# Softplus of dt in a state-space scan: its last sum moved from GpSimd to VectorE, its bias moved into the product

## The chip, the cores and the metric

The kernel runs on one core of a Trainium2 chip. A core has five engines that run beside each other, each with a queue of its own: TensorE (PE, matrix products, with a separate weight load, PEld), VectorE (DVE), ScalarE (ACT), GpSimd (POOL) and SyncE (SP, which here issues nearly all transfers). SBUF is the working memory of 128 partitions; PSUM is the smaller memory that PE writes its products to. The metric is the device time of one execution in microseconds (us), and the time of a kernel is the median of its runs. All numbers are fp32 throughout.

## The reference

Four images of 384 channels and 32 x 32 pixels pass two layers. The first begins with a selective scan (a state-space model) over each image in four directions k, with 16 states for each channel. Cut to what matters:

```python
xs = _cross_scan(x)                                   # 4 directions, each (384, 1024)
x_dbl = einsum('bkdl,kcd->bkcl', xs, x_proj_weight)   # 44 rows: 12 dts, 16 B, 16 C
dts = einsum('bkrl,kdr->bkdl', dts, dt_projs_weight)  # 12 -> 384
A = -exp(A_logs)
dt = softplus(dts + dt_projs_bias[None, :, :, None])
# for each position l:   h = h * exp(dt * A) + (dt * u) * B ;  y = sum over n of h * C
ys = ys + Ds * u
x = x + gelu(layernorm(_cross_merge(ys)))
```

After it come a mixture of four experts (each token takes two of them, hidden width 1536), an attention layer with eight heads, and a last two-layer product. In this document these three, with the routing and combining around the experts, are called the tail of an image.

## The kernel before

**The scan.** Work is cut into 32 units: image b (4), direction k (4) and half i (2) of the 1024 positions, 512 positions in each. A unit is cut into three chunks c of 128 channels. For a chunk, `chunk` (L388) loads dt and dt*u from memory in a layout where a partition is a pair of channel and state (`dtr`, L401 to L406), and then, four times, for 4 of the 16 states (g), and for two pairs (q): POOL multiplies dt*u by B (`bx`, L419), ACT takes the exponential of dt times A into a PSUM tile (`da`, L428, two buffers), DVE runs the recurrence along the positions (the scan, L433). The product with C is made by POOL for q = 0 (L447) and by DVE for q = 1 (L440). PE sums over states with a selection matrix into `acc` (L454), and DVE adds that to `y` (L281, L285). There are six buffers of `bx`, which come free when PE has read them.

**The projection.** `project` (L292) prepares the next unit while the present one is scanned: it is a generator that `scan_layer` steps forward once after each group of four states. It multiplies the input with `wx` to 44 rows (`xd_ps`, L317), copies them to SBUF (`xd`, L321), sends the B and C rows through memory to be spread over partitions (`bcs`), and then for each chunk calls `begin`: PE multiplies 12 rows with `wdt` into the PSUM tile `dt_ps` (L344), and softplus follows. It is written as relu(v) + ln(1 + e) with e = exp(-|v|), v being the product plus the bias, and one term more. That term is the rounding error of 1 + e: `one_e` is the rounded sum 1 + e, and ln(1 + e) is better given by ln(one_e) - ((one_e - 1) - e). So the sum has four parts: relu, ln(one_e), -(one_e - 1) and e.

The first image and the others differ in how they sum it. For image 0, PE does it with four identity products (L357), since no other work claims PE then. For images 1 to 3 ACT makes relu in place in `dt_ps` (L349) and `one_e - 1` (L361); POOL makes the two differences (L374, L375), and DVE adds the last to `dt_ps` (L381). In both cases DVE then multiplies by the input (L382), ACT copies dt out of PSUM (L383), and SP sends both to memory (`dd`, L384 and L385), from where `chunk` loads them for the next unit. The bias comes in through the bias operand of ACT's Abs and Relu (L348, L349), from a column of the constants `cols`.

**PSUM.** `dt_ps`, `acc`, `xd_ps` and the two tiles of each layer norm share one tag with two buffers (`psum`, tag "ps").

**The order.** While image b is scanned, the tail of image b - 1 is put among its instructions: `between` calls `tail_batch`, with `route` (L603), `experts` (L836: L906 and L921 on PE), `combine` (L932: two diagonal tiles by POOL, L942, and 16 gathers by POOL, L951), `attention` (L989: L1030 and L1076 on PE) and `last_layers` (L1089). The program text doesn't fix the order of a queue: when the kernel is built, a scheduler works it out for every engine from the dependencies, from priorities and from its own estimate of each instruction's time. Each queue is then fixed. Three things in the text bind it further: in `project` the sums are placed behind the last POOL or DVE instruction of the state group before (`behind`), parts of the tail carry a higher priority, and the tail of image 3 has nothing beside it but what the tail of image 2 has left.

Of the kernel before, what the change touches and what calls it, by code (L numbers as in the profile page):

```python
# [9 lines left out]
F32 = mybir.dt.float32  # L10
I32 = mybir.dt.int32
AF = mybir.ActivationFunctionType
ALU = mybir.AluOpType
# [4 lines left out]
P = 128  # L18
B = 4
D = 384  # L20
DC = D // P
HW = 32
L = HW * HW
HF = 512
NH = L // HF

KG = 4
ORDER = (0, 1, 3, 2)
NS = 16
R = 12  # L30
XD = R + 2 * NS
# [28 lines left out]

_COLS = [
    ("alog", KG * NB * NG),
    ("dtb", KG * DC),
    ("ds", KG * DC),
    ("lnw", DC),
    ("lnb", DC),
# [22 lines left out]
class Room:  # L89


    def __init__(self, tc, ctx, name, bufs):
        self.tc, self.name, self.bufs = tc, name, bufs
        self.sb = ctx.enter_context(tc.tile_pool(name=name, bufs=1, reuse_waits="tile"))
# [14 lines left out]
def halves(i):  # L109
    return slice(i * HF, (i + 1) * HF)  # L110


class Body:
    def __init__(self, ctx, tc, a):
        self.tc, self.nc, self.a = tc, tc.nc, a
        nc = self.nc
        const = ctx.enter_context(tc.tile_pool(name="const", bufs=1))
        self.const = const


        nc.scalar.preload_act_table_set("natural_log_exp_and_others")
        self.cols = const.tile([P, NCOL], F32, tag="cols", name="cols")
        nc.scalar.dma_start(out=self.cols, in_=a["cols"])

        self.ident = const.tile([P, P], F32, tag="ident", name="ident")
        make_identity(nc, self.ident)
        self.ones = const.tile([P, P], F32, tag="ones", name="ones")
        nc.gpsimd.memset(self.ones, 1.0)
        self.eps5 = const.tile([P, 1], F32, tag="eps5", name="eps5")
        nc.gpsimd.memset(self.eps5, 1e-5)  # L130
        self.eps6 = const.tile([P, 1], F32, tag="eps6", name="eps6")
        nc.gpsimd.memset(self.eps6, 1e-6)

        self.minus1 = const.tile([P, 1], F32, tag="minus1", name="minus1")
        nc.gpsimd.memset(self.minus1, -1.0)

        self.c2sum = const.tile([P, 1], F32, tag="c2sum", name="c2sum")
        lo, hi = COL["c2"]
        nc.vector.tensor_reduce(self.c2sum, self.cols[:, lo:hi], AX.X, ALU.add)
# [42 lines left out]
    def scan_layer(self, x1, between):  # L182

        nc, tc, a = self.nc, self.tc, self.a
        with ExitStack() as ctx:
            wp = ctx.enter_context(tc.tile_pool(name="s_w", bufs=1))
# [2 lines left out]
            dap = ctx.enter_context(tc.tile_pool(name="s_da", bufs=2, space=PSUM))  # L189
            psum = ctx.enter_context(tc.tile_pool(name="s_ps", bufs=2, space=PSUM))  # L190

            wx = wp.tile([P, DC, KG, XD], F32, tag="wx", name="wx")
            nc.scalar.dma_start(out=wx, in_=a["wx"].rearrange("(c p) k m -> p c k m", p=P))
            nega = wp.tile([P, KG * NB * NG], F32, tag="nega", name="nega")
            lo, hi = COL["alog"]
# [57 lines left out]
            for n, unit in enumerate(units):  # L253
                b, k, i = unit
                fed, ahead = ahead, []
                project = iter(())
                if n + 1 < len(units):
                    nb = units[n + 1][0]
                    if nb not in us:
                        us[nb] = start(nb)  # L260
                    project = self.project(units[n + 1], us[nb], wx, work, dram, psum, ahead)
                    next(project)
# [4 lines left out]
                for c in range(DC):  # L267
# [5 lines left out]
                    if k % 2 == 0:  # L273
                        ys = y[:, c, halves(i)]
                        out = acc
                    else:
                        w = slice(i * (HW // NH), (i + 1) * (HW // NH))
                        ys = y[:, c, :].rearrange("p (h w) -> p h w", h=HW)[:, :, w]
                        out = acc.rearrange("p (w h) -> p h w", h=HW)
# [12 lines left out]
    def project(self, unit, u, wx, work, dram, psum, made):  # L292

        nc, a = self.nc, self.a
        b, k, i = unit
        by_cols = k % 2 == 1
        w = slice(i * (HW // NH), (i + 1) * (HW // NH))  # L300

        def part(c):
            if by_cols:
                return u[:, c, :].rearrange("p (h w) -> p w h", h=HW)[:, w, :]
            return u[:, c, halves(i)]

        def split(ap):
            return ap.rearrange("p (w h) -> p w h", h=HW) if by_cols else ap

        def k2(name, shape=(P, HF)):  # L310
            return work.tile([*shape], F32, tag="k2", name=name, bufs=6)

        wdt = k2("wdt", (R, D))
        nc.sync.dma_start(out=wdt, in_=a["wdt"][:, k, :])
        ps = psum.tile([P, HF], F32, tag="ps", name="xd_ps")
        for c in range(DC):
            nc.tensor.matmul(  # L317
                split(ps[:XD, :]), wx[:, c, k, :], part(c), start=(c == 0), stop=(c == DC - 1)
            )
        xd = k2("xd", (XD, HF))  # L320
        nc.scalar.copy(xd, ps[:XD, :])  # L321
        rows = dram.tile([2 * NS, HF], F32, tag="rows", name="rows")
        nc.sync.dma_start(out=rows, in_=xd[R:XD, :])
        view = rows.rearrange("(t g n) l -> n t g l", t=2, g=NG)
        bcs = []
        for g in range(NG):
            bc = work.tile([P, 2, HF], F32, tag="bcs", name="bcs", bufs=5)
            for n in range(NJ):
                nc.sync.dma_start(
                    out=bc[n * DB : (n + 1) * DB], in_=view[n, :, g].partition_broadcast(DB)  # L330
                )
            bcs.append(bc)

        dd = dram.tile([2, D, HF], F32, tag="dd", name="dd")
        made += [bcs, dd]
        yield  # L340

        def begin(c):
            ps = psum.tile([P, HF], F32, tag="ps", name="dt_ps")
            nc.tensor.matmul(ps, wdt[:, c * P : (c + 1) * P], xd[:R, :], start=True, stop=True)  # L344
            bias = self.col("dtb", k * DC + c)
            mag, one_e, lnw = k2("mag"), k2("one_e"), k2("lnw")
            relu = k2("relu") if b == 0 else ps
            nc.scalar.activation(mag, ps, AF.Abs, bias=bias)  # L348
            nc.scalar.activation(relu, ps, AF.Relu, bias=bias)  # L349
            nc.scalar.activation(mag, mag, AF.Exp, scale=-1.0)  # L350
            nc.scalar.activation(one_e, mag, AF.Identity, bias=1.0)
            nc.scalar.activation(lnw, one_e, AF.Ln)
            if b == 0:
                nc.scalar.activation(one_e, one_e, AF.Identity, bias=1.0, scale=-1.0)
                terms = [lnw, one_e, mag, relu]
                for t in terms:
                    nc.tensor.matmul(  # L357
                        ps, self.ident, t, start=(t is terms[0]), stop=(t is terms[-1])
                    )
            else:  # L360
                nc.scalar.activation(one_e, one_e, AF.Identity, bias=self.minus1)  # L361
            return ps, mag, one_e, lnw

        def behind(engine):
            if self.place_behind is None:
                return nullcontext()
            return self.tc.issue_after(self.place_behind[engine])

        for c in range(DC):
            ps, mag, one_e, lnw = begin(c)  # L370
            yield
            if b > 0:
                with behind("pool"):
                    nc.gpsimd.tensor_sub(mag, one_e, mag)  # L374
                    nc.gpsimd.tensor_sub(lnw, lnw, mag)  # L375
            yield
            d, du = mag, one_e
            rows = slice(c * P, (c + 1) * P)
            with behind("dve"):
                if b > 0:  # L380
                    nc.vector.tensor_add(ps, ps, lnw)  # L381
                nc.vector.tensor_mul(split(du), split(ps), part(c))  # L382
            nc.scalar.copy(d, ps)  # L383
            nc.sync.dma_start(out=dd[0, rows, :], in_=d)  # L384
            ins = nc.sync.dma_start(out=dd[1, rows, :], in_=du).ins  # L385
        made.append(ins)
# [602 lines left out]
    def attention(self, xc, sums, room):  # L989
# [68 lines left out]

        steps = [(t, i, j) for t in range(HEADS // 2) for i in range(NH) for j in range(MB)]
        made = [project(0)]  # L1060
        ahead = scores(0, made[0][0], 0, 0, None)
        atts = []
# [292 lines left out]
def layouts(inputs):  # L1355

    i = {k: np.asarray(v) for k, v in inputs.items()}

    def vec(v, lead):
        return np.moveaxis(v.reshape(*lead, P, -1), len(lead), 0).reshape(P, -1)  # L1360
# [2 lines left out]
        "alog": np.ascontiguousarray(  # L1363
            i["L0_conv_A_logs"].reshape(KG, NB, DB, NG, NJ).transpose(4, 2, 0, 1, 3)
        ).reshape(P, -1),
        "dtb": vec(i["L0_conv_dt_projs_bias"], (KG, DC)),
        "ds": vec(i["L0_conv_Ds"], (KG, DC)),
        "lnw": vec(i["L0_conv_ln_weight"], (DC,)),
        "lnb": vec(i["L0_conv_ln_bias"], (DC,)),
# [7 lines left out]
    arrays = {  # L1377
        "x": i["x"].reshape(B, D, L),
        "cols": np.concatenate([packed[n] for n, _ in _COLS], axis=1),
        "wx": i["L0_conv_x_proj_weight"].transpose(2, 0, 1),  # L1380
        "wdt": i["L0_conv_dt_projs_weight"].transpose(2, 0, 1),
        "wg": i["L0_ffn_gate_w"],
        "bg": i["L0_ffn_gate_b"],
        "w1": i["L0_ffn_w1"].reshape(NE, DC, P, HID).transpose(0, 2, 1, 3),
# [6 lines left out]
            axis=2,  # L1391
# [9 lines left out]
            axis=1,  # L1401
# [7 lines left out]
            axis=1,  # L1409
# [19 lines left out]
```

## Time and profile before

| what | value |
|---|---|
| median of 3 runs | 4389.3 us (4378.26 to 4389.32) |
| profiled execution, its own time | 4365.25 us |
| its span, first to last instruction | 4363.5 us |
| busy PE | 3382.3 us (78%) |
| busy POOL | 3049.6 us (70%) |
| busy DVE | 2919.3 us (67%) |
| busy ACT | 2504.0 us (57%) |
| mean granted clock of PE | 0.86 |
| DMA moved | 684.74 MB |

The profile is of one execution. A busy time is the union of an engine's instructions; a span's stretches are named by their start and end in us. In a row of the groups view stand the line of the kernel, the engine, the operation, output and inputs by the program's names, shapes, the count after an x, then busy time in us, mean ns of one, and the idle time of the engine just before these instructions with what ended it. A row of the waits view says who waited for whom, and then the total in us, how often, and the longest. A row of the stretches gives start and end, length, busy time of PE, weight load, DVE, ACT and POOL, each with a count, then the granted clock of PE, the share of the DMA engines and GB/s.

### The profile page before, as it was taken

To read this page: it belongs to the slowest core of one execution; us is meant where nothing else is said; L and a number is where in the kernel's file an instruction comes from. 1 tells how busy PE (TensorE), PEld (TensorE's weight loads), DVE (VectorE), ACT (ScalarE), POOL (GpSimd) and SP (SyncE) were. 2 spreads that over 40 slices of the span, in tenths; PEclk is the share of its full clock that TensorE was granted. 3 is DMA by queue.
4 is the path that set the end of the run, shared out by engine and by line. 5 is a ranking of instruction groups with operands and counts; after the bars stand their busy time and mean duration, and the time that the engine had idled before them with its cause. 6 is when DMAs were issued, how large, how long until landed. Compare 5 with 4: busy or idle time off the path is not lost. (4 is left out here: it accounts for less than half of the span.)

```text
span 4363.5 us, 46084 instructions
## 1 busy us (share of the span) xinstructions
PE 3382.3 (78%) x13436; PEld 1581.3 (36%) x13436; DVE 2919.3 (67%) x4331; ACT 2504.0 (57%) x4470; POOL 3049.6 (70%) x1475
## 2 busy tenths in 40 slices
PE   6545544379997895579997888579998799999896
PEld 2111111145553221235554322135554234666323
DVE  5888888967877868968787867968887740200102
ACT  4445545556665875466575777466666564343353
POOL 5999998898988968688898978789898831000100
PEclk7766776589997997779998999679999899999997
DMA  5444354577886534457779534457789434336200
GB/s 136 114 122 116 106 162 115 151 228 214 231 241 183 142 109 139 125 174 213 213 229 279 154 95 132 115 158 225 215 233 273 134 108 142 116 126 214 63 17 15
DMA packets 404756, 684.74 MB, mean 157 GB/s; under 512 B 50960, under 2 KB 206480, under 8 KB 404496
## 3 DMA queue, kind: packets, MB, share of 16 engines
q1 hardware_dynamic: 395184, 655.37, 51.9%
q0 software_dynamic: 8192, 25.17, 1.7%
q8 instruction: 108, 1.77, 0.2%
q14 instruction: 152, 1.25, 0.1%
q10 hardware_dynamic: 1120, 1.18, 0.1%
HBM read 561.47 MB, written 120.06 MB: 156 GB/s over the span
## 5 line engine op out<-in xcount | busy, mean ns | idle before, releaser
L419 POOL TENSOR_TENSOR bx<-dtr,bcs 128x1024 f32<-128x1024 f32 x768 | 1792.4, 2361 | 229.6 <-PE acc L454 118.7
L428 ACT ACTIVATE da<-dtr,nega 128x512 f32<-128x512 f32 x1536 | 1045.3, 690 | 945.8 <-DVE bx L440 564.3
L447 POOL TENSOR_TENSOR bx<-bx,bcs 128x1024 f32<-128x1024 f32 x384 | 903.1, 2359 | 179.1 <-DVE carry L444 74.3
L906 PE MATMUL h_ps<-xc,w 128*128 128x256 f32 (+1 forms) x3168 | 675.0, 368 | 60.8 <-DMA w<-in_w 18.7
L454 PE MATMUL acc<-bx,sel 128*32 128x512 f32 x3072 | 496.8, 697 | 289.2 <-POOL bx L447 232.4
L921 PE MATMUL y_ps<-w,hs 128*128 128x384 f32 x1824 | 643.2, 505 | 38.1 <-ACT hs L914 37.8
L906 PEld LDWEIGHTS h_ps<-xc,w 128*128 128x128 f32 x3168 | 556.1, 200 | 238.7 <-issue 112.8
L433 DVE TENSOR_TENSOR_SCAN bx<-da,carry,bx 128x512 f32<-128x512 f32 x384 | 474.7, 1270 | 129.3 <-ACT da L428 65.8
L433 DVE TENSOR_TENSOR_SCAN bx<-da,bx 128x512 f32<-128x512 f32 x384 | 453.3, 1210 | 117.1 <-POOL bx L419 59.2
L433 DVE TENSOR_TENSOR_SCAN da<-da,carry,bx 128x512 f32<-128x512 f32 x384 | 478.0, 1274 | 66.5 <-ACT da L428 60.9
L440 DVE TENSOR_TENSOR bx<-da,bcs 128x512 f32<-128x512 f32 x768 | 510.3, 680 | 3.7
L433 DVE TENSOR_TENSOR_SCAN da<-da,bx 128x512 f32<-128x512 f32 x384 | 456.2, 1219 | 63.3 <-ACT da L428 53.0
L921 PEld LDWEIGHTS y_ps<-w,hs 128*128 128x128 f32 x1824 | 350.0, 196 | 325.8 <-issue 78.2
L1036 ACT ACTIVATE ex<-s_ps 128x512 f32<-128x512 f32 x512 | 300.8, 592 | 156.6 <-PE s_ps L1030 154.4
L1030 PE MATMUL s_ps<-w 64*128 64x512 f32 x1024 | 307.9, 662 | 53.1 <-ACT ex L1036 51.8
L911 ACT ACTIVATE hs<-h_ps,bb 128x256 f32<-128x256 f32 (+1 forms) x528 | 201.0, 441 | 218.8 <-PE h_ps L906 218.4
L1076 PE MATMUL o_acc<-ex,vt 128*64 128x512 f32 x1024 | 287.0, 638 | 18.1 <-ACT ex L1036 11.5
L454 PEld LDWEIGHTS acc<-bx,sel 128*32 128x32 f32 x3072 | 80.0, 116 | 585.9 <-POOL bx L447 319.8
L942 POOL TENSOR_TENSOR diag<-ident,g_weight 128x1024 f32<-128x1024 f32 x8 | 15.0, 1893 | 345.6 <-PE xc_ps L889 331.0
L925 DVE TENSOR_TENSOR y<-y_ps,bb 128x384 f32<-128x384 f32 x76 | 41.7, 549 | 273.4 <-PE y_ps L921 273.4
L344 PE MATMUL dt_ps<-xd,wdt 12*128 12x512 f32 x192 | 123.2, 726 | 71.4 <-ACT mag L383 43.8
L1030 PEld LDWEIGHTS s_ps<-w 64*128 64x128 f32 x1024 | 82.8, 190 | 256.0 <-ACT ex L1036 206.0
(214 smaller groups left out, 3767.2 us busy)
## 6 DMA issues: line engine op xcount, KB each, us to landing
w<-in_w SPq DMA_DIRECT2D x352, 576.0 KB
dtr<-dd SPq DMA_DIRECT2D x1536, 128.0 KB
bcs<-rows SPq DMA_DIRECT2D x512, 128.0 KB
dd<-one_e SPq DMA_DIRECT2D x96, 256.0 KB
dd<-mag SPq DMA_DIRECT2D x96, 256.0 KB
rows<-zero SPq DMA_DIRECT2D x76, 192.0 KB
xs<-rows SPq DMA_DIRECT2D x32, 384.0 KB
made<-y SPq DMA_DIRECT2D x32, 384.0 KB
```

Source lines behind the costliest of these rows:

```text
L419: pool = nc.gpsimd.tensor_mul(bx, dtr[q][1], bc[:, 0].unsqueeze(1).to_broadcast([P, 2, HF])).ins
L428: nc.scalar.activation(da, dtr[q][0][:, j, :], AF.Exp, scale=nega[:, col : col + 1])
L433: nc.vector.tensor_tensor_scan(run(h), run(da), run(bx[:, j, :]), 0.0 if first else hold, ALU.mult, ALU.add,)
L440: dve = nc.vector.tensor_mul(bx[:, j, :], h, cg).ins
L447: pool = nc.gpsimd.tensor_mul(bx, bx, cg.unsqueeze(1).to_broadcast([P, 2, HF])).ins
L454: nc.tensor.matmul(acc[lo : lo + DB, :], sel, out[q][:, j, :], start=(g == 0), stop=(g == NG - 1),)
L906: nc.tensor.matmul(ps[:, r, :], w1[(f + r) // wf][:, c, (f + r) % wf * P : ((f + r) % wf + 1) * P], xc[:, c, :], start=(c == 0), stop=(c = ...
L911: nc.scalar.activation(hs[:, f + r, :], ps[:, r, :], AF.Identity, bias=bb[:, f + r : f + r + 1])
L921: nc.tensor.matmul(out[:, :D], hs[:, f, t * P : (t + 1) * P], w2[f // wf][:, f % wf, :], start=(f == 0), stop=(f == FC - 1),)
L1030: ins = nc.tensor.matmul(ps, w[rows, j * P : (j + 1) * P], w[rows, halves(i)], start=True, stop=True).ins
L1036: done.append(nc.scalar.activation(ex[:, o, :], ps, AF.Exp, scale=HD**-0.5, accum_out=sums[:, t, 2 * j + o, i : i + 1],).ins)
L1076: ins = nc.tensor.matmul(out[cols, :], made[t][1][:, j, cols], ex[:, o, :], start=(j == 0), stop=(j == MB - 1),).ins
```

## The change

The bias of dt enters through the product. `wx` gets a column of zeros, so that `xd` has a 45th row of zeros, to which ACT adds 1 as it copies (an Identity with a column of the identity matrix as its bias). `wdt` gets 32 rows of zeros, against the B and C rows, and the bias as its 45th row. The dt product runs over all 45 rows. The bias columns and the constant -1 are gone.

For images 1 to 3, ACT makes neither relu nor `one_e - 1`, and POOL makes no difference. DVE sums in three steps in `dt_ps`, each a scalar_tensor_tensor: max(v, 0) + lnw, then (one_e - 1) - that, then -that + e. Image 0 keeps its four products on PE and its relu.

```diff
-            wx = wp.tile([P, DC, KG, XD], F32, tag="wx", name="wx")
+            wx = wp.tile([P, DC, KG, XD + 1], F32, tag="wx", name="wx")
...
-        wdt = k2("wdt", (R, D))
+        wdt = k2("wdt", (XD + 1, D))
...
-                split(ps[:XD, :]), wx[:, c, k, :], part(c), start=(c == 0), stop=(c == DC - 1)
+                split(ps[: XD + 1, :]), wx[:, c, k, :], part(c), start=(c == 0), stop=(c == DC - 1)
...
-        xd = k2("xd", (XD, HF))
-        nc.scalar.copy(xd, ps[:XD, :])
+        xd = k2("xd", (XD + 1, HF))
+        nc.scalar.activation(
+            xd, ps[: XD + 1, :], AF.Identity, bias=self.ident[: XD + 1, XD : XD + 1]
+        )
...
-            nc.tensor.matmul(ps, wdt[:, c * P : (c + 1) * P], xd[:R, :], start=True, stop=True)
-            bias = self.col("dtb", k * DC + c)
+            nc.tensor.matmul(ps, wdt[:, c * P : (c + 1) * P], xd, start=True, stop=True)
             mag, one_e, lnw = k2("mag"), k2("one_e"), k2("lnw")
-            relu = k2("relu") if b == 0 else ps
-            nc.scalar.activation(mag, ps, AF.Abs, bias=bias)
-            nc.scalar.activation(relu, ps, AF.Relu, bias=bias)
+            nc.scalar.activation(mag, ps, AF.Abs)
+            if b == 0:
+                relu = k2("relu")
+                nc.scalar.activation(relu, ps, AF.Relu)
...
-            else:
-                nc.scalar.activation(one_e, one_e, AF.Identity, bias=self.minus1)
...
+        def stt(out, a, scalar, b, op0, op1):
+            nc.vector.scalar_tensor_tensor(out, a, scalar, b, op0=op0, op1=op1)
+
...
-            if b > 0:
-                with behind("pool"):
-                    nc.gpsimd.tensor_sub(mag, one_e, mag)
-                    nc.gpsimd.tensor_sub(lnw, lnw, mag)
             yield
...
                 if b > 0:
-                    nc.vector.tensor_add(ps, ps, lnw)
+                    stt(ps, ps, 0.0, lnw, ALU.max, ALU.add)
+                    stt(ps, one_e, 1.0, ps, ALU.subtract, ALU.subtract)
+                    stt(ps, ps, -1.0, mag, ALU.mult, ALU.add)
                 nc.vector.tensor_mul(split(du), split(ps), part(c))
```

Since the order of every queue is worked out anew when the program is built, instructions that the diff doesn't name can stand elsewhere in it too.

More of the change, by code (lines that the diff above doesn't have):

```diff
@@ L62 @@
     ("alog", KG * NB * NG),
-    ("dtb", KG * DC),
     ("ds", KG * DC),
@@ L132, in __init__ @@
         nc.gpsimd.memset(self.eps6, 1e-6)
-        self.minus1 = const.tile([P, 1], F32, tag="minus1", name="minus1")
-        nc.gpsimd.memset(self.minus1, -1.0)
         self.c2sum = const.tile([P, 1], F32, tag="c2sum", name="c2sum")
@@ L1365, in layouts @@
         ).reshape(P, -1),
-        "dtb": vec(i["L0_conv_dt_projs_bias"], (KG, DC)),
         "ds": vec(i["L0_conv_Ds"], (KG, DC)),
@@ L1379, in layouts @@
         "cols": np.concatenate([packed[n] for n, _ in _COLS], axis=1),
-        "wx": i["L0_conv_x_proj_weight"].transpose(2, 0, 1),
-        "wdt": i["L0_conv_dt_projs_weight"].transpose(2, 0, 1),
+        "wx": np.pad(i["L0_conv_x_proj_weight"].transpose(2, 0, 1), ((0, 0), (0, 0), (0, 1))),
+        "wdt": np.concatenate(
+            [
+                i["L0_conv_dt_projs_weight"].transpose(2, 0, 1),
+                np.zeros((2 * NS, KG, D), np.float32),
+                i["L0_conv_dt_projs_bias"].reshape(1, KG, D),
+            ],
+            axis=0,
+        ),
         "wg": i["L0_ffn_gate_w"],
```

## The prediction

> **What bounds the kernel now.** I read the page's busy shares first: PE 78%, POOL 70%, DVE 67%, ACT 57%. No engine is full, so I cut the span at the points where the work changes. The answers for stretches:
>
> ```profile
> 44.00:774.00 730.00, 382.83 (x1104) 98.74 (x1104) 636.78 (x854) 378.22 (x593) 674.94 (x296) 0.69 0.46 124
> 774.00:1673.00 899.00, 729.78 (x3027) 346.85 (x3019) 702.86 (x1011) 577.12 (x1065) 773.36 (x377) 0.89 0.65 186
> 1673.00:2609.00 936.00, 746.83 (x3035) 367.60 (x3035) 735.98 (x1083) 587.85 (x1009) 771.38 (x377) 0.87 0.62 181
> 2609.00:3526.00 917.00, 743.94 (x3083) 362.98 (x3085) 728.39 (x1069) 581.14 (x1008) 776.62 (x375) 0.89 0.62 180
> 3526.00:4363.50 837.50, 749.65 (x3151) 394.52 (x3149) 108.31 (x293) 362.44 (x770) 51.48 (x39) 0.93 0.31 103
> ```
>
> After the length come busy times of PE, weight load, DVE, ACT and POOL. Row one is the scan of image 0, with nothing beside it: POOL is 92% busy. Rows two to four scan images 1 to 3 while the tail (experts, attention, last layers) of the image before runs among them: 2752 us together, POOL 2321 (84%), PE 2220 (81%), DVE 2167 (79%), ACT 1746 (63%). Row five is what the tail has left when the last scan is over; PE is busy for 90% of it and sets the end. So the span is scan stage plus remaining tail, and the change can move the border between them.
>
> Within the scan stage two regimes alternate. In the expert stretches PE is fullest:
>
> ```profile
> 905.00:1332.00 427.00, 400.29 (x1695) 239.06 (x1693) 339.89 (x462) 275.31 (x441) 366.81 (x170) 0.95 0.80 230
> 1945.00:2365.00 420.00, 389.94 (x1662) 233.26 (x1663) 334.57 (x454) 275.55 (x436) 361.39 (x167) 0.96 0.79 230
> 2983.00:3290.00 307.00, 285.15 (x1183) 171.17 (x1182) 251.13 (x323) 199.83 (x311) 273.66 (x128) 0.96 0.78 224
> ```
>
> That is 1154 us with PE 93%, POOL 87%, DVE 80%. The other 1598 us of the stage (by subtraction) have POOL 83%, DVE 78%, PE 72%. The waits inside 774 to 3521 us say what holds POOL and DVE there (total, times, longest):
>
> ```profile
> POOL bx L419 <- PE acc L454: 102.5, 31, 15.1
> POOL mag L374 <- ACT one_e L361: 49.0, 16, 7.7
> ...
> DVE bx L433 <- ACT da L428: 109.0, 126, 5.1
> DVE da L433 <- ACT da L428: 105.5, 58, 5.9
> DVE bx L433 <- POOL bx L419: 93.4, 58, 8.2
> ...
> DVE dt_ps L381 <- POOL lnw L375: 18.1, 6, 8.9
> ```
>
> The largest idle time of DVE is for ACT's da (214 us), not for POOL (105 us): a lighter POOL frees DVE of the smaller part only.
>
> [...] POOL waits 49 us at L374 with bx multiplies standing behind it. [...] Each new instruction has one input in PSUM; L381, of that kind, shows 662/687/700 ns (minimum, median, maximum) beside a busy POOL, no blocking. [...]
>
> **The change part by part.** Prices come from the groups view:
>
> ```profile
> L375 POOL TENSOR_TENSOR lnw<-lnw,mag 128x512 f32<-128x512 f32 x72 | 92.3, 1282 | 0.4
> L374 POOL TENSOR_TENSOR mag<-one_e,mag 128x512 f32<-128x512 f32 x72 | 91.8, 1274 | 56.0 <-ACT one_e L361 49.0 <-DMA dtr<-dd 6.9
> L361 ACT ACTIVATE one_e<-one_e,minus 128x512 f32<-128x512 f32 x72 | 51.8, 720 | 0.8
> L381 DVE TENSOR_TENSOR dt_ps<-dt_ps,lnw 128x512 f32<-128x512 f32 x72 | 49.4, 686 | 18.8 <-POOL lnw L375 18.8
> L349 ACT ACTIVATE dt_ps<-dt_ps,cols 128x512 f32<-128x512 f32 x72 | 47.0, 653 | 0.0
> ```
>
> - POOL loses L374 and L375: 91.8 + 92.3 = 184 us of work, and up to 56 us of waiting before L374.
> - ACT loses L361 and, for images 1 to 3, L349: 51.8 + 47.0 = 99 us. Abs without a bias column may be 49 ns shorter (677 against the 628 of L350): 72 x 49 = 3.5 us. ACT is nowhere the fullest engine; what this buys is earlier da.
> - DVE gets three scalar_tensor_tensor for one add. The nearest row is L164, the same operation on PSUM and SBUF, 680 ns; the strided L281 has 737. 72 x 3 x 680 - 49.4 = +97 us (+110 at 737). They follow each other on one tile; L382, which depends on L381, starts 0.03 us after its end, so I add no gap.
> - PE: 45 rows in place of 12 in the dt product, 45 columns in place of 44 in xd. Rows don't show in a time: 12 rows with 512 columns take 726 ns, the 128-row L454 takes 697. Nothing. The wider wdt load (69 KB for 18 KB, 32 times, on SP's queue) and the wx and column loads: nothing, as the loads for a unit go out one unit, some 100 us, ahead[...].
> - The wait moves: the first of the three stands in DVE's queue on ACT's Ln, where L381 stood on POOL. Behind it are scans, and behind these ACT's da and POOL's second multiply. Bounds: nothing, if Ln is done; 72 x 1.2 us = 86 us if DVE each time comes two ACT instructions early. L381 waited 0.25 us on average; I take 0.2 us, 15 us in all, inside the choice below.
>
> What the diff doesn't tell: the order of every queue is worked out when the program is built, and it moves. Counting POOL's 1152 scan multiplies as a clock, image 0's route moves from after 317 to 329, image 1's route from 623 to 659, image 2's from 929 to 1010, and image 2's combine, at 1109 before, now comes after all 1152. Each scan unit has less tail beside it, and more tail is left at the end. On PE, behind the last L454, stood one image of experts, one combine and prologue and 1.7 images of attention; now there are 1.31, 2 and 2.0. Priced by the groups: experts 0.31 x (675.0 + 643.2)/4 = 102 us, combine 15.8, prologue 4.8, attention with its projections 66: about 191 us of PE time. The last stretch has PE near full, so this lengthens it, less what fits into its holes: from 4000 to 4100 PE is idle for 22 us while image 3 combines alone, and the new order puts image 2's last layers there. **Remaining tail: +165 us** (bounds 125 and 205).
>
> **What the scan stage gives back.** Its loads become PE 2220 - 191 = 2029 (-8.6%); POOL 2321 - 184 - 19 (the combine's two diagonals and 16 gathers) = 2118 (-8.8%); DVE 2167 + 97 - 18 (tail work gone) = 2246 (+3.7%). DVE becomes the fullest: 2246 of 2752.
>
> Expert stretches, in shares of the old time: PE 93 to 85, POOL 87 to 79, DVE 80 to 83. If the fullest engine keeps its fill, the time falls with it, 8.6%: -99 us. If time goes with the sum of the three, 260 to 247, it falls 5%: -58. I take -70. Other stretches: POOL 83 to 75, DVE 78 to 81. By the fullest engine, 82.6 to 80.6, 2.4%: -39 us; if POOL alone set the pace, 8.8%: -140. I take -55, near DVE's end, because the da waits stay. **Scan stage: -125 us.**
>
> Sum: 4363.5 - 125 + 165 = 4403.5 us of span, +40. The profiled execution took 4365.25, the runs have a median of 4389.3; the difference carries over: **4429 us**.
>
> **Rivals.**
> - *POOL and PE paced everything* (faster). Then the scan stage gives 99 + 140 = 239, and 239 - 165 = 74 us are won: 4315. For it: POOL has the largest share in the stage, its 56 us of waiting go too, and PE, in order, held bx for 102.5 us; where PE is full, work taken out and done at the end is only moved, not added. Against it: DVE would run at 2246 of 2513, 89%, with the da waits and the tail's own waits in its queue; alone with image 0 it reached 87%. It decides when the stage shortens by over 165 us, 6%.
> - *DVE's queue pays* (clearly slower). The Ln wait nears its 86 us bound, or DVE's 97 us come on top where it is already dense at image boundaries; the stage then gives some 45 us: 4389 + 120 = 4509.
> - *The change does not do what it says* (the row of ones is lost, or the sum has a wrong sign) would show in the values, not in the time: the instructions are the same.
>
> **Chances.** Mine 0.52 (4379 to 4470), the faster rival 0.32 (4300 to 4379), DVE's queue 0.16 (4470 to 4520). A measurement here can't tell less than 0.3%, 13 us, from no change. Faster 0.33, same 0.09 (the edges where stage and tail cancel), slower 0.58. The range leaves out a tenth on each side: 4318 to 4505.
>
> **What would show it.** POOL's busy time near 2866, ACT's near 2400, DVE's near 3017, with three instructions of 0.68 us. The last L454 near 3400, not 3526: that is the scan stage's -125. Behind it near 1000 us of tail, PE full until image 3 is alone. DVE's waits for da the largest, its waits for POOL mostly gone. Wrong if the last L454 comes before 3361 (faster), if DVE waits long for Ln (third case), or if PE idles in the last stretch after image 2's combine.

## The result

The changed kernel is slower by about half a per cent: 4410.03 us (median of 6 runs) against 4386.21 us of the kernel before (6 runs on the same chip), a ratio of 1.0056 with a 95% interval of 1.0043 to 1.0069. The forecast was 4429 us, slower. The profiled span went from 4363.5 to 4407.2 us. (The profile of before was not taken beside these runs: its execution took 4365.25 us, 0.5% less than the 4386 us measured here. So the two spans differ by 44 us where the medians differ by 24, and some 20 us in the comparison of lengths below are not the change's.)

The stretches of the changed kernel, cut at the same places: the scan of image 0, the scan stage of images 1 to 3, and what is left of the tail after the last `acc` product (length, then busy PE, weight load, DVE, ACT, POOL):

```profile
44.00:769.00 725.00, 386.20 (x1104) 99.58 (x1108) 638.11 (x858) 371.60 (x586) 668.18 (x291) 0.70 0.48 125
769.00:3388.00 2619.00, 2117.78 (x8447) 994.58 (x8444) 2201.57 (x3262) 1595.76 (x2780) 2133.40 (x969) 0.87 0.64 182
3388.00:4407.20 1019.20, 918.91 (x3844) 481.89 (x3844) 125.17 (x331) 433.14 (x931) 70.39 (x57) 0.93 0.34 111
```

Before, the stage was 2752 us and the rest 837.5. So the stage gave 133 us and the rest took 182, and image 0 gave 5: the sum is the 44 us by which the spans differ. (An estimate that first scales the lengths of before by 4386.21/4365.25: the stage gave 146, the rest took 178, image 0 gave 9.) DVE is now the fullest engine of the stage (2202 of 2619, 84%; before, 79%), POOL has 81%. The groups of the sum, by form:

```profile
L366 DVE SCALAR_TENSOR_TENSOR dt_ps<-dt_ps,lnw 128x512 f32<-128x512 f32 x72 | 49.5, 687 | 37.8 <-ACT lnw L350 37.7
L366 DVE SCALAR_TENSOR_TENSOR dt_ps<-one_e,dt_ps 128x512 f32<-128x512 f32 x72 | 49.4, 687 | 0.8
L366 DVE SCALAR_TENSOR_TENSOR dt_ps<-dt_ps,mag 128x512 f32<-128x512 f32 x72 | 49.2, 683 | 0.5
L344 ACT ACTIVATE mag<-dt_ps 128x512 f32<-128x512 f32 x96 | 56.2, 585 | 25.6 <-PE dt_ps L342 24.0 <-PE dt_ps L355 1.6
```

Three steps of 0.69 us, the first with 38 us of waiting for ACT's Ln. The first waits of POOL in the scan stage:

```profile
POOL bx L444 <- DVE bx L430: 102.4, 41, 6.9
POOL bx L444 <- DVE carry L441: 97.3, 39, 6.3
POOL bx L416 <- PE acc L451: 89.7, 27, 28.0
```

L444 is POOL's second multiply (by C), L447 before. It waits 200 us for DVE. Before, from 774 to 3521 us, the same two rows made 125 us:

```profile
POOL bx L447 <- DVE carry L444: 66.7, 31, 6.5
POOL bx L447 <- DVE bx L433: 58.6, 31, 8.2
```

So 75 of the 184 us that POOL was spared it now spends waiting for the engine that took the work.

### The profile page after: what moved, and what is told of

Read it like the earlier page. It is cut to its first block, busy times and chain, and to the rows that moved or that the text cites. A ratio compares the mean times of both kernels' runs of the same rounds, so it can differ in the third digit from the quotient of the medians.

```text
span 4407.2 us, 45776 instructions
## 1 busy us (share of the span) xinstructions
PE 3450.9 (78%) x13436; PEld 1586.2 (36%) x13436; DVE 2972.2 (67%) x4475; ACT 2417.7 (55%) x4324; POOL 2873.6 (65%) x1330
## 5 line engine op out<-in xcount | busy, mean ns | idle before, releaser
L444 POOL TENSOR_TENSOR bx<-bx,bcs 128x1024 f32<-128x1024 f32 x384 | 904.1, 2360 | 273.1 <-DVE bx L430 112.1
L451 PE MATMUL acc<-bx,sel 128*32 128x512 f32 x3072 | 545.9, 720 | 327.4 <-POOL bx L444 275.2
L430 DVE TENSOR_TENSOR_SCAN da<-da,bx 128x512 f32<-128x512 f32 x384 | 456.3, 1219 | 41.7 <-ACT da L425 32.2
L1114 POOL TENSOR_TENSOR xt<-xt,wb 128x3072 f32<-128x3072 f32 x4 | 26.8, 6698 | 607.7 <-DMA wb<-in_wb 607.7
L342 PE MATMUL dt_ps<-xd,wdt 45*128 45x512 f32 x192 | 128.8, 757 | 59.3 <-ACT mag L380 55.0
```

The lines of the kernel that those rows point to most:

```text
L430: nc.vector.tensor_tensor_scan(run(h), run(da), run(bx[:, j, :]), 0.0 if first else hold, ALU.mult, ALU.add,)
L444: pool = nc.gpsimd.tensor_mul(bx, bx, cg.unsqueeze(1).to_broadcast([P, 2, HF])).ins
L451: nc.tensor.matmul(acc[lo : lo + DB, :], sel, out[q][:, j, :], start=(g == 0), stop=(g == NG - 1),)
```

## The experiments

Three theories went in. *Border*: the loss comes from where the tail stands, since PE time costs its full length behind the scan and less inside it. *Conservation*: it costs the same on either side. *VectorE*: DVE's added steps take back what POOL gave. A fourth, *order or queue* (a queue order worked out anew can itself lose or win time), was added after the first four runs. All ratios are to the kernel before, timed on the same chip beside the run; the lengths are from each run's own profile. Before has a median of 4386 us beside the changed kernel and of 4358 to 4362 us beside the other runs. The lengths of "changed" are therefore some 0.6% long against the other rows (scaled by 4358/4386, an estimate: image 0 764, stage 2602, rest 1013, stage + rest 3615); the ratios don't have this fault, and where the two disagree, the ratios count.

| run | ratio, 95% interval | image 0 | stage | rest | stage + rest |
|---|---|---|---|---|---|
| before | 1 | 774 | 2752 | 837.5 | 3590 |
| changed | 1.0056, 1.0043 to 1.0069 | 769 | 2619 | 1019 | 3638 |
| border_back | 1.0110, 1.0095 to 1.0126 | 767 | 2778 | 864 | 3642 |
| pool_load_back | 1.0019, 1.0011 to 1.0027 | 779 | 2742 | 841 | 3583 |
| bias_row_only | 0.9940, 0.9927 to 0.9954 | 774 | 2703 | 844 | 3547 |
| dve_sum_only | 1.0046, 1.0032 to 1.0060 | 773 | 2595 | 1015 | 3610 |
| order_nudge | 0.9996, 0.9989 to 1.0002 | 770 | 2751 | 830 | 3581 |
| bias_row_zero | 0.9896, 0.9880 to 0.9911 | 746 | 2745 | 830 | 3575 |
| no_correction | 0.9922, 0.9910 to 0.9934 | 770 | 2537 | 1020 | 3557 |
| shared_sum | 0.9979, 0.9970 to 0.9989 | 775 | 2595 | 978 | 3573 |
| late_product | 0.9950, 0.9936 to 0.9963 | 747 | 2567 | 1015 | 3582 |
| late_before | 0.9910, 0.9895 to 0.9925 | 749 | 2761 | 811 | 3572 |
| late_shared | 0.9907, 0.9892 to 0.9922 | 744 | 2677 | 895 | 3572 |
| late_bias | 0.9888, 0.9872 to 0.9904 | 750 | 2744 | 821 | 3565 |

**The border put back.** On the changed kernel:

```diff
-        self.experts(b, self.slots, room)
+        with self.tc.high_priority(offset=1600):
+            self.experts(b, self.slots, room)
```

> The changed kernel, with one thing more: the experts of an image get a scheduling priority 1600 steps higher, so that the built order puts them earlier among the scan of the next image. No work is added or taken. Behind the last acc product PE now has 1.0 image of experts, 1 combine and 1.73 images of attention, as in the kernel before (1.0, 1, 1.7), where the changed kernel has 1.31, 2 and 2.0. Border theory (the loss comes from where the tail stands: PE time moved behind the scan costs its full length there, but only part of it inside the scan, where PE has idle time): the rest after the scan falls from 1019 us to about 840, the scan stage grows from 2618 us by 60 to 120, the time is 4290 to 4350 us, ratio to before 0.978 to 0.992. Conservation theory (PE is full in the expert stretches, so work put there costs as much as at the end): scan stage +180, time 4400 to 4420, ratio 1.003 to 1.008. VectorE theory (its 97 us more are what costs): the same, 1.003 to 1.008.

Measured 1.0110, outside all three ranges of the ratio. (Its 4407 us lie within the conservation theory's 4400 to 4420, but before took only 4358 us beside it.) The stages of this run:

```profile
767.00:3545.00 2778.00, 2276.66 (x9093) 1075.08 (x9095) 2222.56 (x3300) 1657.36 (x2929) 2153.76 (x988) 0.88 0.62 181
3545.00:4409.00 864.00, 768.90 (x3201) 400.21 (x3197) 109.59 (x294) 369.73 (x784) 51.56 (x39) 0.91 0.30 101
```

The rest fell by 155 us and the stage grew by 159 (149 and 176 against the scaled lengths). The border theory falls: the tail costs at least its whole length inside the scan too. The conservation theory, with its 180 us, comes nearest, but by the ratios putting the tail back even cost 0.5%, some 24 us, which it doesn't explain. How it slows the scan is in the waits of this run:

```profile
POOL bx L416 <- PE acc L451: 218.1, 43, 22.6
POOL bx L444 <- DVE bx L430: 125.4, 44, 6.9
POOL bx L444 <- DVE carry L441: 105.0, 43, 7.2
DVE xc L891 <- PE xc_ps L887: 87.6, 22, 10.7
DVE y L923 <- PE y_ps L919: 67.2, 12, 11.4
```

With the experts back among the scan, POOL waits 218 us for PE to release `bx`, not 90. And there is a second reading: with the border of the kernel before and less POOL work than it, the stage is 2778 us where before had 2752. In all, the change did not shorten the stage once the border was held. This run has a fault as a test, though. The priority moved the experts' steps in DVE's queue as well: DVE waits 155 us for the experts' products (the last two rows, to 3390 us) where before it waited 54. What POOL's relief alone is worth is better read from no_correction, below.

**GpSimd's load put back.** On the changed kernel, two subtractions into a spare tile:

```diff
             yield
+            if b > 0:
+                with behind("pool"):
+                    spare = k2("spare")
+                    nc.gpsimd.tensor_sub(spare, one_e, mag)
+                    nc.gpsimd.tensor_sub(spare, lnw, mag)
             yield
```

> The changed kernel, with two GpSimd subtractions of 128x512 put back in their old places, which write a spare tile that nobody reads (extra work, 184 us of GpSimd). VectorE keeps its three steps (+97 us), ScalarE stays relieved (-102 us). The built order has the border of the kernel before: 1.0 image of experts, 1 combine, 1.77 of attention behind the last acc product. Border theory: the border follows GpSimd's load alone, the time comes to about that of the kernel before, ratio 0.995 to 1.008, with the last acc product near 3526 us. VectorE theory (its work adds to a stage that it shares with GpSimd): 60 to 110 us slower than before, ratio 1.014 to 1.025.

Measured 1.0019, in the border theory's range, with the last `acc` product at 3521 us: POOL's load sets the border in the built order, as that theory's first half said. The VectorE theory missed: with POOL's load and the border as before, DVE's 97 us more, beside ScalarE's 102 us less, cost 0.2% (some 8 us) and not 60 to 110 us. That 184 us of useless POOL work make the changed kernel faster (1.0019 for 1.0056, intervals apart) was foreseen by no theory. Against border_back, on the same chip and with nearly the same border, they make it faster by 0.9%. The two differ in that work and in the order of the queues; it stays open, and is taken up at the end.

**The parts alone.** In bias_row_only only the wider product and the bias-free Abs and Relu are kept; in dve_sum_only only the two further VectorE steps (before: L361, L374 and L375):

```diff
-                nc.scalar.activation(one_e, one_e, AF.Identity, bias=self.minus1)
...
-                    nc.gpsimd.tensor_sub(mag, one_e, mag)
-                    nc.gpsimd.tensor_sub(lnw, lnw, mag)
...
                     nc.vector.tensor_add(ps, ps, lnw)
+                    nc.vector.scalar_tensor_tensor(
+                        ps, one_e, 1.0, ps, op0=ALU.subtract, op1=ALU.subtract
+                    )
+                    nc.vector.scalar_tensor_tensor(
+                        ps, ps, -1.0, mag, op0=ALU.mult, op1=ALU.add
+                    )
```

> One part alone: the bias enters by the 45th row of the dt product and ScalarE's Abs and Relu lose their bias column; the sum stays as before, with relu and one_e - 1 on ScalarE, two differences on GpSimd and one add on VectorE. The border is that of the kernel before (1.0, 1, 1.78). All theories: no change beyond what a new order does, ratio 0.996 to 1.004, about 4386 us. A rival that the wider product or its loads cost: above 1.005.

> The other part alone: bias by ScalarE's Abs and Relu as before, relu stays on ScalarE in place, the two GpSimd differences and ScalarE's one_e - 1 are replaced by two more VectorE steps. GpSimd -184 us, ScalarE -52 us, VectorE +97 us. The built order has the border of the changed kernel (1.31 experts, 2 combines, 2.0 attention). Border theory: like the changed kernel, ratio 1.003 to 1.012, scan stage some 10 to 20 us longer than 2618 for 47 us more on ScalarE. If the bias row was what cost: ratio at or below 1.000.

The bias row alone is faster, 0.9940, just outside what was expected; the sum alone is slower, 1.0046, as expected, though its stage (2595) didn't come out longer than that of the changed kernel. So the loss is the sum's. Over bias_row_only, the changed kernel is slower by 1.2% (1.0056 / 0.9940).

**Is it the order?** order_nudge is the kernel before with `high_priority(offset=1000)` round the experts: another PE order, the same queue on POOL. bias_row_zero is bias_row_only with a column of zeros as the bias of Abs and Relu.

> The kernel before, with no work added or taken: the experts get a scheduling priority 1000 steps higher. GpSimd's queue keeps its order and the border stays (1.0 experts, 1 combine, 1.7 attention after the last acc product); some 180 of PE's instructions stand elsewhere. Order theory (after border_back fell: any newly worked-out order moves the time by up to half a per cent[...]): outside 0.998 to 1.002, either way, up to 0.006. Load theory (only work on VectorE, GpSimd and ScalarE counts): 0.998 to 1.002.

> bias_row_only (0.994) with a column of zeros as the bias of ScalarE's Abs and Relu, so that these cost what they cost in the kernel before (677 and 653 ns for 588 and 592; 11 us in all in the stage). The built order is a third one, not that of bias_row_only and not that of before; the border is that of before (1.0, 1, 1.67). Load theory (the 11 us of ScalarE, on which VectorE's scans wait, made the 26 us): 0.998 to 1.002. Order theory: anything from 0.994 to 1.006, and not tied to the 11 us.

order_nudge is 0.9996, as the load theory had it: not every new order counts. bias_row_zero is 0.9896, outside both ranges, and 28 us of its 42 us in span are in image 0 (746 for 774). There its POOL runs without a gap; from 136 to 630 us:

```profile
136.00:630.00 494.00, 260.02 (x782) 63.90 (x782) 458.75 (x607) 267.10 (x417) 493.73 (x215) 0.67 0.50 132
```

Before, in six like units (136 to 663 us, 527 us), POOL was busy for 500. What differs is POOL's own order. Between a first multiply and the second one on the same `bx` stand three other first multiplies in 65 of image 0's 96 cases here, in 29 before; one alone in 5 here, in 31 before. With one, POOL can come to the second multiply before DVE has done its scan, and stands with first multiplies queued behind it: up to 663 us POOL waited 12 us for DVE there before, and 16 us for PE at the first multiplies; in bias_row_zero, to 640 us, 2.6 and 1.3. Behind image 0 the picture is the other way round: stage and rest take 3575 us, 28 more than in bias_row_only. Whether the 11 us of ACT or the new order made these 28 us isn't parted.

**VectorE's steps taken away.** The changed kernel without the rounding correction, so a part of the computation is left out:

```diff
                     stt(ps, ps, 0.0, lnw, ALU.max, ALU.add)
-                    stt(ps, one_e, 1.0, ps, ALU.subtract, ALU.subtract)
-                    stt(ps, ps, -1.0, mag, ALU.mult, ALU.add)
```

> The changed kernel without its second and third VectorE step: the rounding correction of ln(1 + e) is left out, dt is max(v, 0) + lnw. VectorE has one step of 0.69 us as in the kernel before, GpSimd has none (-184 us), ScalarE -102 us. The border is that of the changed kernel (1.29 experts, 2 combines, 2.0 attention). VectorE theory (VectorE's 97 us take back what GpSimd's 184 us give): scan stage shorter by 50 to 100 us than the changed kernel's 2619, ratio 0.980 to 0.993. PE theory (PE's work and its idle time set the whole, and neither engine's load is what fills them): 0.999 to 1.008, as the changed kernel.

Measured 0.9922, inside VectorE's range:

```profile
770.00:3307.00 2537.00, 2078.08 (x8474) 978.63 (x8471) 2110.86 (x3120) 1593.70 (x2780) 2131.30 (x968) 0.89 0.65 188
3307.00:4327.00 1020.00, 911.95 (x3812) 476.01 (x3808) 124.64 (x330) 432.50 (x929) 70.46 (x57) 0.92 0.33 110
```

The border and the POOL and ACT work are those of the changed kernel, DVE has 91 us less, and the profiled stage is 82 us shorter. A part of the 82 is not the edit's, since the two profiles were not taken side by side: by the ratios (1.0056 to 0.9922) the whole kernel gained 1.3%, about 59 us. So some 0.6 us of time were paid for each us of DVE's two steps.

The run also shows what the relief of POOL is worth. The stages of bias_row_only:

```profile
774.00:3477.00 2703.00, 2198.24 (x9045) 1058.87 (x9043) 2172.20 (x3155) 1723.70 (x3053) 2320.49 (x1125) 0.89 0.62 186
3477.00:4321.00 844.00, 765.92 (x3247) 395.86 (x3245) 110.74 (x297) 371.79 (x797) 51.52 (x39) 0.95 0.30 102
```

Both have the bias row and one DVE step of 0.69 us. no_correction lacks POOL's 184 us and 94 us of ACT, and has the border of the changed kernel. It comes out at 0.9922 for 0.9940, with intervals that overlap, and stage and rest are 3557 us for 3547. So, as far as one order of each can tell, the relief won a few tenths of a per cent at most, and DVE's two added steps cost 1.3%: that is the changed kernel's loss against bias_row_only, taken apart.

**The sum shared.** POOL adds lnw and e, DVE takes two steps:

```diff
+                with behind("pool"):
+                    nc.gpsimd.tensor_add(lnw, lnw, mag)
...
-                    stt(ps, ps, -1.0, mag, ALU.mult, ALU.add)
+                    stt(split(du), split(ps), -1.0, part(c), ALU.mult, ALU.mult)
...
+                nc.scalar.mul(d, ps, -1.0)
```

> The sum shared: GpSimd adds lnw and e (one operation of 1.28 us for two), VectorE takes two steps for three, the sign goes into ScalarE's copy and VectorE's product with the input. Against the kernel before GpSimd has -92 us, VectorE +49, ScalarE -102. The border lies between (1.18 experts, 2 combines, 2.0 attention). VectorE theory: better than both kernels, 0.990 to 0.998. PE theory: 0.998 to 1.006. Order theory: within half a per cent of 1.000, with no sign to be told.

0.9979: better than both kernels, barely. It is at the upper edge of VectorE's range and within the order theory's too, so it doesn't decide between them. Against the changed kernel, taking one DVE step away won 0.8%, although POOL got 92 us back.

**POOL's queue bound.** Four kernels have the second multiply traced behind both first multiplies of the next state group:

```diff
+        ahead = by_b(0)          # both first multiplies (L416) of a group
         for g in range(NG):
+            now = ahead
+            if g + 1 < NG:
+                ahead = by_b(g + 1)
...
-                    pool = nc.gpsimd.tensor_mul(
-                        bx, bx, cg.unsqueeze(1).to_broadcast([P, 2, HF])
-                    ).ins
+                    with self.tc.issue_after(ahead[1][1]):
+                        pool = nc.gpsimd.tensor_mul(
+                            bx, bx, cg.unsqueeze(1).to_broadcast([P, 2, HF])
+                        ).ins
```

> The changed kernel with GpSimd's queue bound further: its multiply by C (the second one, which waits for VectorE's scan) goes behind both first multiplies of the next state group, so that 3 first multiplies stand between a bx and its second multiply in 225 of 288 cases of images 1 to 3 (before: 144) and in 71 of 96 of image 0 (26). No work is added or taken; the border is that of the changed kernel (1.30, 2, 2.0). Queue theory (GpSimd's relief is lost because it waits at the second multiply, in order, for a VectorE that is now fuller: 200 us in the changed kernel for 123 before): image 0 falls from 769 to about 745 us, as where that order came by chance, the 200 us fall below 120, the scan stage falls from 2619 by 40 to 90, ratio to before 0.980 to 0.993. VectorE theory (VectorE itself is the pace, the waits only mirror it): image 0 gains up to 25 us, the stage stays within 20 us of 2619, ratio 0.998 to 1.005.

> The kernel before with the same binding of GpSimd's queue (3 between in 236 of 288 and 73 of 96). Border as before (1.0, 1, 1.56). Queue theory: image 0 from 774 to about 746, the stage from 2752 by 20 to 50 (its waits there are 123 us), ratio 0.982 to 0.990. VectorE theory: GpSimd sets the pace here, its waits are time lost, so the same, 0.982 to 0.992. What tells them apart is the pair: if late_product comes out at or below late_before, the sum on VectorE pays once the queue lets it; if late_product stays over late_before by 0.5% or more, VectorE's added work is what costs.

> The shared sum (one GpSimd add, two VectorE steps, sign in the copy and the product) with the same binding of GpSimd's queue. Border 1.0 experts, 2 combines, 2.0 attention. Both theories: better than shared_sum's 0.998 by image 0's 25 us, at most 0.992; queue theory 0.978 to 0.988.

> The bias row with the sum as before (GpSimd two differences, VectorE one add) and the same binding of GpSimd's queue. Border 1.0, 1, 1.62. As bias_row_only had 0.994 with image 0 at 774 us, both theories give 0.980 to 0.989 here; a candidate for the fastest. Against late_before it shows once more what the bias row is worth: 0.998 to 1.000 of it if only its 11 us of ScalarE count.

Image 0 falls to 744 to 750 us in all four: that gap was POOL's queue. In the stage of late_product POOL's first waits are

```profile
POOL bx L416 <- PE acc L463: 98.1, 39, 9.7
POOL bx L416 <- issue: 77.4, 13, 22.9
POOL bx L456 <- DVE bx L441: 71.3, 27, 8.4
POOL bx L456 <- DVE carry L452: 55.2, 28, 9.7
```

L456 is the second multiply: 127 us for 200, not quite the 120 forecast. The stage falls by 52 us to 2567, in the queue theory's range, but only by 35 us against the scaled 2602, which is short of it; the ratio, 0.9950, lies between the ranges of the two theories. On the kernel before, the same binding leaves the stage as it was (2761 for 2752), though the waits at its second multiply (L459) fall from some 125 to 45 us. From 750 to 3360 us:

```profile
POOL bx L419 <- issue: 136.0, 20, 17.3
POOL bx L459 <- DVE bx L444: 22.7, 7, 8.4
POOL bx L459 <- DVE carry L455: 22.2, 6, 6.3
```

POOL now stands elsewhere (the first row: 136 us for 12), so a wait that is gone from one line is not yet time won. Behind image 0, the binding changed stage + rest by -33 us (changed kernel, scaled), -18 (before), -1 (shared sum) and +18 (bias row). The gain in image 0 is thus shown four times over; behind it, a new order moves the time by up to some 30 us either way, and that the second multiply's waits were a cost there isn't shown.

The pair answers the other question: bound alike, the sum on DVE still costs. late_product is over late_before by 0.4% (0.9950 for 0.9910, intervals apart), just under the 0.5% set, and over late_bias, which differs from it in the sum alone, by 0.6%. In the free order it was 1.2%; the difference lies within what orders alone moved, so it can't be put down to one cause. late_shared, with one DVE step less than late_product, is 0.4% faster, for 0.8% in the free order.

late_bias (0.9888), bias_row_zero (0.9896), late_shared (0.9907) and late_before (0.9910) are the fastest with the whole computation. Their intervals overlap, so none is shown to be the fastest. Of the forecasts, late_before met that of the VectorE theory and missed that of the queue theory by 0.001, late_bias met the one given for both, and late_shared stayed under its bound of 0.992 but not in the queue theory's range.

## Why the prediction was right or wrong

- **Sign, size, range: right.** Forecast +40 us, 4429; measured +24, 4410, within 4318 to 4505. It is a small difference of two large terms, and one of these came out near for a wrong reason (below), so the nearness is in part luck.
- **Prices.** The three steps have 684 to 690 ns at the median (680 taken). POOL's busy time is 2873.6 (2866), ACT's 2417.7 (2400). Abs lost 92 ns with its bias column, not 49. DVE's busy time is 2972, not 3017: the new groups add 148.1 - 49.4 = 98.7 us as priced, but others shrank by 22 us together (among them L1138, a product with two SBUF inputs, by 9), and the remaining 24 us are records that overlap, which a busy time counts once. Nothing was put for the 45 rows of the dt product, and nothing shows in its median: 693 ns (587 to 1219) for 692 before with 12 rows (587 to 1217). The mean, 757 for 726, rose, as did that of `acc` (720 for 697, below).
- **Ln at the head of DVE's queue:** 38 us, where 15 was taken and 86 was the bound.
- **"Remaining tail: +165 us": +182, within its bounds.** The 22 us that were to fit into a hole did not: PE is idle for 100 us in the rest (1019.2 - 918.9), before for 88 (837.5 - 749.7). PE's work there grew by 169 us, not by the 191 priced (whose parts, as listed, add up to 189). So two errors, 22 us in the work and 34 in the idle time, cancelled in part.
- **"Scan stage: -125 us": -133, but for the wrong cause.** This is the step that failed. The forecast gave 70 us to lower loads of PE and POOL in the expert stretches and 55 to POOL's relief in the others, with DVE's 97 us counted only as a limit on the second. border_back shows that with the tail back the stage is 26 us longer than before: the shortening went with the tail that had left it. And no_correction against bias_row_only shows that POOL's and ACT's relief, with the border moved, won some 0.2%. The loads were off too: PE's busy time in the stage was to be 2029 us and is 2118, as its products ran longer. Right was the remark, under the faster rival, that work taken out where PE is full is only moved; drawn to its end it makes the border cost nothing, and leaves the loss to be explained by something else.
- **What explains it.** DVE's two added steps cost about 59 us of time for 91 us of work (no_correction, by the ratios), where I had counted on POOL's and PE's fall to outweigh them. Two smaller pairs agree in sign: one step less won 0.8% (shared_sum) and 0.4% (late_shared). How it is paid is less clear. In the changed kernel POOL's second multiply, which waits for DVE, stood 200 us for 125, but in late_before 80 us less of such waits won nothing in the stage. The rival "DVE's queue pays" named the engine, but priced it as too far out at +120 us, and gave Ln and image boundaries as the places; the wait that grew most was POOL's second multiply, which I had not priced.
- **The rival "POOL and PE paced everything"** needed over 165 us from the stage; it gave 133.
- **Signs given:** the last `acc` product was to come near 3400 (3388), the rest near 1000 us (1019). DVE's largest wait was to be that for da: it is (74.0 + 50.7 = 125 us in the stage, before 214). Its waits for POOL were to be mostly gone, but 84 us of 105 remain.

Open: why 184 us of useless POOL work make the changed kernel faster by 0.4%, and why in that run DVE's added steps cost next to nothing over the kernel before. POOL waits less at its second multiply there, and the orders are other ones, but order and load were not parted: a queue order of one with the load of the other was not tried. So DVE's steps are shown to cost in the changed kernel, and not in every order. Open too: what the bias row is worth. It is 0.6% in the free order, but stage and rest of bias_row_only are the shortest of all runs with the whole computation, and in the bound order (late_bias and late_before) the intervals overlap.

## What to carry to other kernels

Before crediting an engine's relief, ask which engine takes the work, how full that one is in the same stage, and what queue stands waiting for it: here DVE at 79% of the stage took 98 us, and the two added steps cost some 59 us of time, while 184 us less of a fuller POOL won next to nothing. In a kernel whose queue order is worked out when it is built, split the span at the borders between stages before comparing: a stage that became shorter may only have sent its work to the next one. A run that puts the border back tests it, if one looks what else it moved. Compare lengths of profiles only where the unchanged kernel takes the same time beside both; here before itself differed by 0.6% between two sets of runs, as much as the change's whole effect. And look at the order of the queue itself: a multiply that waits for another engine, placed two instructions later, won 0.9% on the kernel before, more than the change studied lost.

## What the runs showed of the hardware

- A column as the bias of ACT's Abs and Relu on 128x512 cost time over none: Abs 677 ns with (before), 585 (changed) and 588 (bias_row_only) without; Relu 653 with (before), 592 without (bias_row_only). In bias_row_zero, which adds nothing but a column of zeros to these two, ACT is busy for 2488 us over image 0, stage and rest, in bias_row_only for 2470. Two rows of bias_row_only:

```profile
L347 ACT ACTIVATE mag<-dt_ps 128x512 f32<-128x512 f32 x96 | 56.4, 588 | 46.1 <-PE dt_ps L345 34.2 <-DMA rows<-zero 8.4 <-issue 1.8
L349 ACT ACTIVATE dt_ps<-dt_ps 128x512 f32<-128x512 f32 x72 | 42.6, 592 | 0.0
```

- The same 3072 `acc` products took 697 ns on average before, 720 in the changed kernel (545.9 us of PE for 496.8), with the same operands:

```profile
L454 PE MATMUL acc<-bx,sel 128*32 128x512 f32 x3072 | 496.8, 697 | 289.2 <-POOL bx L447 232.4 <-ACT mag L383 21.6 <-ACT sc L699 12.6
L451 PE MATMUL acc<-bx,sel 128*32 128x512 f32 x3072 | 545.9, 720 | 327.4 <-POOL bx L444 275.2 <-DVE y L281 24.8 <-DVE bx L437 10.1
```

So PE's busy time isn't a fixed amount of work. It doesn't simply follow PE's waits for POOL: before has 232 us of these and 697 ns, bias_row_only 212 us and 703. Within before, the products up to 774 us took 865 ns at a granted clock of 0.70, and those of the stage 644 ns at 0.88. The small change of the stage's clock (0.87 for 0.88) is less than that of its products (677 ns for 644), so it alone doesn't explain the change; the rest is open.

- One DVE product with two SBUF inputs (L1138 before, 128x256) took longer where a POOL instruction ran beside it. Of its 16 cases before, the six with one beside them took 1298 to 2558 ns, the longest ending 0.3 us after the POOL multiply; the ten without took 409 to 425 ns. In the changed kernel (L1135) none of the 16 met a POOL instruction, and all took 403 to 426 ns. The eight of the stage before, then all 16 after:

```profile
L1138 DVE TENSOR_TENSOR z<-zt,rstd 128x256 f32<-128x256 f32 x8 | 12.2, 1580 | 0.0
L1135 DVE TENSOR_TENSOR z<-zt,rstd 128x256 f32<-128x256 f32 x16 | 5.7, 413 | 4.1 <-ACT rstd L145 3.6 <-DVE zt L1132 0.5
```

The steps of the new sum, with one input in PSUM, keep to 666 to 700 ns throughout, 667 to 700 in the 191 of 216 cases with a POOL instruction beside them. Whether it is the place of the inputs that makes the difference was not tried.
